# Layer 1's first norm, keys and values of image 0 placed inside layer 0's last image

## The chip, the cores and the metric

The kernel runs as one program on one core of a Trainium2 chip. The metric is the device time of one execution in microseconds (us); less is better. The core's engines each work through their own instructions in program order: TensorE (PE in the profile, with PEld for its weight loads), VectorE (DVE), ScalarE (ACT), GpSimd (POOL) and SyncE (SP, which issues most of the transfers here). They wait for each other by semaphores. Matrix products are written to PSUM, in eight banks; everything else lies in SBUF.

## The reference

Eight images of 256 channels by 32 by 32 pixels go through two layers, all in float32. Layer 0 is a convolutional block, layer 1 a causal attention and a mixture of eight experts over the 1,024 pixels of an image as tokens.

```
# layer 0, per image x [256, 1024]
a = rmsnorm(x) -> 1x1 conv to q, k (4 heads x 32) and v (4 heads x 64), batch norms folded
o = softmax(q.T k) v  +  depthwise 3x3 conv of v
x = x + gamma1 * proj(o)
h = 1x1 conv of rmsnorm(x) to 1024 channels ; depthwise 3x3 conv       # 8 groups of 128 channels
h = gelu(h[:512]) * h[512:]                                              # 4 products of two groups
x = x + gamma2 * irfft2(rfft2(1x1 conv of h to 256) * filter)           # on 8x8 blocks

# layer 1, per image t [1024, 256]
z = layernorm(t)
W = (z WQ.T)(z WK.T).T / 16 ;  A = causal softmax of W, rows where W == 0 left out
t = t + A (z WV.T)
t = t + sum over 8 experts of gate_e * expert_e(layernorm(t))            # two hidden layers, relu
```

## The kernel before

The program has three parts, one after the other: layer 0 for the images 0 to 7, layer 1's attention for the images 0 to 7 (the function `tokens`, its block `l1`), and the experts (its block `l2`). Between layers an image lies in DRAM: `t_d[b]` after layer 0, `u_d[b]` after layer 1's attention.

**How the order is made.** Nearly all instructions go through a small recorder, `InOrder`, with one object for each engine (`pe`, `dve`, `act`, `pool`). It keeps an engine's instructions in the order in which the Python code issues them, so that order is written out by hand: stages are generators that issue a few instructions and yield an estimate in us, and `weave`, `together`, `level`, `some` and `silent` interleave them. All recorded instructions carry the recorder's line, L73; groups in the profile are told apart by the names of their tiles. A stage that is issued earlier stands ahead in every engine's queue.

**Layer 0's opening.** SP issues the loads of the weights and of images 0 and 1. `queries_keys(0)`, `stack(0)` and `values(0)` make image 0's attention inputs, and `queries_keys(1)` those of image 1: TensorE products `pq`, evicted by ScalarE to `hi` and by VectorE to `lo`, both stored to DRAM as `part`. `stack(b)` loads them back into `qst` and `kst`. `hi` and `lo` have one buffer each, so the second half of `queries_keys(1)` waits for the store of the first.

**Layer 0's loop.** For each image i, `main_of(i)` runs image i's attention (`attend`: scores `s`, ScalarE's exponentials `pT`, the products `po` and `sums`), its end (`finish`, which divides by the sums in three steps called turn, back and spread, and `project`, products `pp`), and the spectrum of image i-2. Beside it runs `hidden(i - 1)`, the depthwise convolution of the image before: seven or eight groups of eight taps on VectorE, each tap a 128x1024 multiply-add on `x` or `conv`, after TensorE's products `ph` and ScalarE's evictions of them into a padded tile `hpad`. One group in some images goes over TensorE instead (`group_on_pe`: diagonal weights `taps`, products `pc`).

**Layer 0's end, around the change.** Image 7 has no following attention to hide its second half. After `attend(7)` come: the gelus of image 6 on ScalarE woven with `finish(7)` and `project(7)`, then `head`, which weaves `norm2(7)` (tiles `sq`, `ms`, `yr`, `tpy`, `rbn`, `xn`) with `spectrum(6)` (tiles `pz`, `zf`, `pf`, `gf`, `py`); then image 7's convolution alone (`hidden(7, alone=True)`, group 2 on TensorE), with `scores_matrix` on TensorE at its beginning; each product of two finished groups (`hid`) goes at once into the `pz` accumulators (`mix`). `spectrum(7)` closes the layer, and `votes` and `bad` decide whether a fallback runs (it does not for these inputs).

`scores_matrix` turns the two weights WQ and WK (`lin`), multiplies them into one matrix `pa` and stores it as `at_d`. In the kernel before, `lin` takes over the buffer of `qst` after the last attention.

**Layer 1's start.** `tokens` opens its own pools, loads `t`, `at` and `wv` on GpSimd's queue, and then makes image 0's inputs with nothing beside them:

```python
            for _ in first_norm(0):
                pass
            for _ in keys_values(0):
                pass
            load_t(2)
            for b in range(B):
                together(last() if b == B - 1 else causal(b), beside(b), 0.85)
```

`first_norm` calls `layer_norm`: TensorE transposes `tpt`, ScalarE copies them into `zt`, VectorE's statistics `st` and `mv`, six small GpSimd instructions for the reciprocal root `r`, VectorE's scaling of `zt`, transposes back `tpz`, and ScalarE's copies into `z`. `keys_values` multiplies `z` by `at` (`pk`, copied to `kk`) and by `wv` (`pv`, copied to `v`). `causal(b)` then issues image b's scores `s<-kk,z`, and `beside(b)` the next image's norm, keys and values and the last image's second norm.

The pools have fixed places in SBUF. A tile in a place that another tile has held waits for the old tile's last users.

Of the kernel before, what the change touches and what calls it, by code (L numbers as in the profile page):

```python
# [105 lines left out]
def conv_attn_hybrid_kernel(  # L106
# [370 lines left out]
    t = [None] * B  # L477
    with ExitStack() as l0:
        wpool = l0.enter_context(tc.tile_pool(name="w0", bufs=1))
        one = l0.enter_context(tc.tile_pool(name="one0", bufs=1))  # L480
        two = l0.enter_context(tc.tile_pool(name="two0", bufs=2))
        ps_s = l0.enter_context(tc.tile_pool(name="ps_s0", bufs=2, space=PSUM))
# [41 lines left out]
        sel = two.tile([nf, P], F32, tag="pT", name="sel", bufs=4)  # L524
        nc.sync.dma_start(sel, c_sel)
        fp = two.tile([nf, C], F32, tag="pT", name="fp", bufs=4)
# [6 lines left out]
        nc.sync.dma_start(idft, c_idft)  # L533

# [12 lines left out]
        def spread_columns(w, factors, n):  # L547

            diag = two.tile([P, n, P], F32, tag="pT", name="diag", bufs=4)
            sps = ps_m.tile([P, n, P], F32, tag="mm", name="sps")  # L550
            for g in range(n):
                dve.tensor_scalar_mul(diag[:, g, :], ident, factors[:, g : g + 1])
                pe.matmul(sps[:, g, :], ones, diag[:, g, :], start=True, stop=True)
            for k in range(KC):
                dve.tensor_mul(w[:, k, :], w[:, k, :], sps.rearrange("p a b -> p (a b)"))
# [42 lines left out]
        OTHERS = (0, 1, 2, 3, 5, 6, 7, 8)  # L598

# [125 lines left out]
        def stack(b):  # L725
            for g in range(2):
                hi, lo = att[b][g]
                name = ("qst", "kst")[g]
                att[b][name] = st = one.tile([P, NH, N], F32R, tag=name, name=name)
# [6 lines left out]
        def values(b):  # L736


            vT = att[b]["vT"] = one.tile([P, NT, C], F32, tag="vT", name="vT")
# [36 lines left out]
        def attend(b):  # L776
# [76 lines left out]
            for c in range(N // QC):  # L853
                qs = slice(c * QC, (c + 1) * QC)
                po = ps_o.tile([P, NH // 2, QC], F32, tag="po", name="po")
                sm = ps_o.tile([P, QC], F32, tag="sm", name="sums")
                for j0 in range(0, nj, 2):
                    new = []
                    for j in (j0, j0 + 1):
# [4 lines left out]
                        pT = two.tile([P, NH, QC], F32, tag="pT", name="pT", bufs=4)  # L864
# [13 lines left out]
        def finish(b):  # L878
            for step in att[b]["rest"]:
                step()  # L880
                yield 0.4
# [246 lines left out]
        def main_of(i):  # L1128
# [35 lines left out]
            else:  # L1164
                yield from weave(project(i, (0,)), weave(finish(i), gelus, 1), 1)
                yield from project(i, (1,))
# [19 lines left out]
        for _ in queries_keys(1):  # L1186
            pass
        for i in range(B):


            if i == 0:
                level(main_of(i), v_conv(i), SHARE[0])
            else:
                level(main_of(i), hidden(i - 1, v_conv(i)), SHARE[i])

        lin = one.tile([P, 4, KC, C], F32, tag="qst", name="lin")
        for i, src in enumerate((wqT, wkT)):
            nc.sync.dma_start(lin[:, i], src.rearrange("(k p) o -> p k o", p=P))

        def scores_matrix():  # L1200
            for i in range(2):
                tp = ps_m.tile([P, KC, KC, P], F32, tag="mm", name="tpw")
                for g in range(KC):
                    for k in range(KC):
                        pe.transpose(tp[:, g, k, :], lin[:, i, k, g * P : (g + 1) * P], ident)
                act.copy(lin[:, 2 + i], tp.rearrange("p g k d -> p g (k d)"))
                yield 0.5
            pa = ps_m.tile([P, KC, C], F32, tag="mm", name="pa")
            for g in range(KC):
                for k in range(KC):  # L1210
                    pe.matmul(
                        pa[:, g, :], lin[:, 3, k, g * P : (g + 1) * P], lin[:, 2, k, :], start=(k == 0), stop=(k == KC - 1)
                    )
            act.activation(lin[:, 0], pa, AF.Copy, scale=1.0 / math.sqrt(C))
            nc.sync.dma_start(at_d, lin[:, 0])
            yield 1.7

        head = weave(norm2(B - 1), spectrum(B - 2), 1)
# [3 lines left out]
        def rest():  # L1222
            yield from head
            yield from scores_matrix()
# [20 lines left out]
    def tokens(stack):  # L1245
# [11 lines left out]
        mhalf1 = wm.tile([P, NT], F32, name="mhalf1")  # L1257
        nc.gpsimd.memset(mhalf1, -0.5)
# [44 lines left out]
        def layer_norm(src, dst, zt, room, bank):  # L1303

            n = src.shape[2] // P
            mv = room([P, NT, 2], "mv", 2)
            for i0 in range(0, n, 2):
                tp = bank([P, 2, C], "tpt")
                for i in range(2):
                    for k in range(KC):  # L1310
                        c0 = (i0 + i) * P
                        pe.transpose(tp[:, i, k * P : (k + 1) * P], src[:, k, c0 : c0 + P], ident)
                act.copy(zt[:, i0 : i0 + 2, :], tp)
                yield 0.6
                for i in range(i0, i0 + 2):
                    st = room([P, 6], "st", 4)
                    dve.bn_stats(st, zt[:, i, :])
                    dve.bn_aggr(mv[:, i, :], st)
                yield 0.6

            y = room([P, NT], "y1", 2)[:, :n]
            r = room([P, NT], "r1", 2)[:, :n]
            pool.tensor_scalar(y, mv[:, :n, 1], LN_EPS, None, ALU.add)
            pool.tensor_tensor(r, y, mhalf1[:, :n], ALU.pow)
            pool.tensor_mul(y, y, r)
            pool.tensor_mul(y, y, r)
            pool.tensor_scalar(y, y, -0.5, 1.5, ALU.mult, ALU.add)
            pool.tensor_mul(r, r, y)

            for _ in range(4):  # L1330
                yield 1.0

            def scaled(i0):
                for i in range(i0, i0 + 2):
                    dve.tensor_scalar(zt[:, i, :], zt[:, i, :], mv[:, i, 0:1], r[:, i : i + 1], ALU.subtract, ALU.mult)

            scaled(0)
            yield 1.0
            scaled(2)
            yield 1.0  # L1340
            for i0 in range(0, n, 2):
                if i0 + 4 < n:
                    scaled(i0 + 4)
                tp = bank([P, KC, 2, P], "tpz")
                for i in range(2):
                    for k in range(KC):
                        pe.transpose(tp[:, k, i, :], zt[:, i0 + i, k * P : (k + 1) * P], ident)
                act.copy(dst[:, :, i0 * P : (i0 + 2) * P], tp.rearrange("p k i c -> p k (i c)"))
                yield 0.9

# [30 lines left out]
        with ExitStack() as l1:  # L1381
# [8 lines left out]
            def load_t(b, queue=nc.sync):  # L1390
                t[b] = two.tile([P, KC, N], F32, tag="t", name="t1", bufs=3)
                queue.dma_start(t[b], t_d[b])

            load_t(0, pool)
            at = wpool.tile([P, KC, C], F32, name="at")
            pool.dma_start(at, at_d)
            wv_s = wpool.tile([P, KC, C], F32, name="wv")
            pool.dma_start(wv_s, wvT.rearrange("(k p) o -> p k o", p=P))
            feats[1] = wpool.tile([P, KC, HALF], F32, name="feat1")
            load_t(1)  # L1400


            lower = wpool.tile([P, P], F32, name="lower")
            nc.gpsimd.memset(lower, 1.0)
            nc.gpsimd.affine_select(
                out=lower, in_=lower, compare_op=ALU.is_ge, fill=0.0, base=0, pattern=[[-1, P]], channel_multiplier=1,
            )
# [68 lines left out]
            def rows_of_zt():  # L1476
                return two.tile([P, NT, C], F32, tag="zt", name="zt", bufs=1)

            def first_norm(b):
                z[b] = two.tile([P, KC, N], F32, tag="z", name="z1")  # L1480
                yield from layer_norm(t[b], z[b], rows_of_zt(), room, bank)

            def keys_values(b):
                kk = kk_of[b] = two.tile([P, KC, N], F32, tag="kk", name="kk")
                for h in range(2):
                    hs = slice(h * HALF, (h + 1) * HALF)
                    for g in range(KC):
                        pk = ps_m.tile([P, HALF], F32, tag="mm", name="pk")
                        for k in range(KC):
                            pe.matmul(pk, at[:, k, g * P : (g + 1) * P], z[b][:, k, hs], start=(k == 0), stop=(k == KC - 1))  # L1490
                        act.copy(kk[:, g, hs], pk)
                        yield 1.7
                v = v_of[b] = two.tile([P, NT, C], F32, tag="v", name="v")
                for j in range(0, NT, 2):
                    pv = ps_m.tile([P, 2, C], F32, tag="mm", name="pv")
                    for i in range(2):
                        js = slice((j + i) * P, (j + i + 1) * P)
                        for k in range(KC):
                            pe.matmul(pv[:, i, :], z[b][:, k, js], wv_s[:, k, :], start=(k == 0), stop=(k == KC - 1))
                    act.copy(v[:, j : j + 2, :], pv)  # L1500
                    yield 1.7
# [492 lines left out]
```

## Time and profile before

| | us |
|---|---|
| median of 3 runs | 3138.48 (3132.07 to 3140.57) |
| the profiled execution, its own time | 3137.65 |
| its span, first to last instruction | 3135.9 |
| mean granted TensorE clock | 0.966 |
| TensorE busy | 2944.8 (94%) |
| VectorE busy | 2394.8 (76%) |
| ScalarE busy | 1562.0 (50%) |
| GpSimd busy | 314.2 (10%) |
| last `sums` product of image 7's attention ends | 1241.14 |
| first `ph` product of image 7's convolution starts | 1283.70 |
| last product of two groups (`hid`) of image 7 has its first half done | 1375.26 |
| first score product of layer 1 starts | 1417.46 |

The profile comes from one execution. Times inside it count from its first instruction. A row of the timeline gives start, length, engine, source line, operation, output tile and input tiles, shapes, count, and in square brackets the idle time before the row with what ended it. One float32 matrix product appears as two records, one float32 transpose as one. A row of the table by stages gives, for a stretch of time, the busy us of each engine with the number of its instructions in brackets, the granted TensorE clock as a share of full speed, the busy share of the transfer engines, and GB/s.

### The profile page before, as it was taken

How to read it: one execution, taken by the hardware profiler on the slowest of the kernel's cores; microseconds unless marked ns; L12 is line 12 of the kernel's file. 1: busy time of each engine (PE TensorE's matmuls, PEld its weight loads, DVE VectorE, ACT ScalarE, POOL GpSimd, SP SyncE). 2: the span in 40 equal slices, each digit the busy share in tenths (PEclk: the TensorE clock that was granted, in tenths of full speed). 3: DMA queues.
4: the chain of work that ended last, by engine and by line, in shares of the span. 5: the costliest groups of instructions: out<-in, count | busy, mean ns of one | idle time of the engine just before them, and what ended most of it. 6: DMA issues, size and time to landing. Idle time of an engine off the chain costs nothing.

```text
span 3135.9 us, 41559 instructions
## 1 busy us (share of the span) xinstructions
PE 2944.8 (94%) x16802; PEld 1951.5 (62%) x16802; DVE 2394.8 (76%) x3014; ACT 1562.0 (50%) x2312; POOL 314.2 (10%) x422
## 2 busy tenths in 40 slices
PE   7988999999999988869999999899999999999998
PEld 4554555555555555446666666677777777777776
DVE  2387787878787869576776765688888988888887
ACT  3554454545464545323333333465666666666664
POOL 1012111111111110011122222100000000000000
PEclk8999999999999989989999999999999999999999
DMA  5203030303021210012333311411222142112210
GB/s 181 55 1 81 28 82 28 82 28 79 30 74 36 68 28 8 18 67 71 146 120 131 121 78 54 188 68 68 71 91 74 67 167 107 69 68 77 91 68 28
DMA packets 63600, 234.86 MB, mean 75 GB/s; under 512 B 5591, under 2 KB 13607, under 8 KB 54567
## 3 DMA queue, kind: packets, MB, share of 16 engines
q1 hardware_dynamic: 63094, 230.54, 22.1%
q8 instruction: 134, 2.20, 0.3%
q0 software_dynamic: 304, 1.57, 0.1%
q14 instruction: 68, 0.55, 0.1%
HBM read 140.61 MB, written 91.49 MB: 74 GB/s over the span
## 4 chain that ended last, share of the span: by engine, by line
PE 81%; DVE 13%; ACT 3%; issue 1%; DMA 1%; POOL 1%; SPq 0%; ACTq 0%; DVEq 0%; POOLq 0%
PE pm L73 12%; PE pa L73 11%; PE q L73 11%; PE po L73 11%; PE s L73 8%; PE ph L73 6%; DVE o L73 4%; PE sums L73 3%; PE pq L73 3%; PE pz L73 2%; PE pv L73 2%; PE pk L73 2%; DVE conv L73 2%; PE pp L73 2%; DVE x L73 1%
## 5 line engine op out<-in xcount | busy, mean ns | idle before, releaser
L73 PE MATMUL pa<-ze,w 128*128 128x512 f32 x1488 | 423.1, 393 | 0.0
L73 DVE SCALAR_TENSOR_TENSOR x<-hpad,vec,x 128x1024 f32<-128x1024 f32 x248 | 316.7, 1283 | 76.2 <-ACT x L73 68.7
L73 DVE SCALAR_TENSOR_TENSOR conv<-hpad,vec,conv 128x1024 f32<-128x1024 f32 x256 | 328.5, 1287 | 18.3 <-ACT conv L73 12.3
L73 PEld LDWEIGHTS pa<-ze,w 128*128 128x128 f32 x1488 | 278.2, 188 | 63.2 <-issue 3.0
L73 ACT ACTIVATE h<-pa,bn_o,s1a 128x512 f32<-128x512 f32 x256 | 198.6, 776 | 203.2 <-PE pa L73 203.2
L73 ACT ACTIVATE pT<-s 128x1024 f32<-128x1024 f32 x256 | 247.8, 1024 | 98.5 <-PE s L73 98.5
L73 PE MATMUL po<-pT,vT 128*32 128x256 f32 x4096 | 273.5, 385 | 0.0
L73 PE MATMUL q<-h2p,w 128*128 128x512 f32 x768 | 269.0, 459 | 0.0
L73 DVE SCALAR_TENSOR_TENSOR h<-pa,s1b,h 128x512 f32<-128x512 f32 x256 | 191.5, 748 | 93.9 <-PE pa L73 86.8
L73 PE MATMUL ph<-xn,piw 128*128 128x512 f32 x512 | 240.9, 613 | 7.6 <-ACT x L73 4.0
L73 PE MATMUL pm<-h,w 128*128 128x512 f32 x512 | 240.9, 593 | 0.0
L73 PE MATMUL s<-kk,z 128*128 128x512 f32 x512 | 236.8, 594 | 4.1 <-DVE pr L73 4.1
L73 PE MATMUL q<-z_first,w 128*128 128x512 f32 x768 | 217.2, 391 | 2.8 <-DVE z_first L73 1.7
L73 PE MATMUL pm<-h1p,w 128*128 128x512 f32 x768 | 216.7, 390 | 0.5 <-DVE h1p L73 0.5
L73 PEld LDWEIGHTS q<-h2p,w 128*128 128x128 f32 x768 | 144.6, 188 | 83.2 <-issue 59.6
L73 DVE SCALAR_TENSOR_TENSOR o<-vpad,pe_w,o 128x1024 f32<-128x1024 f32 x128 | 163.7, 1283 | 32.0 <-ACT o L73 28.8
L73 PE MATMUL s<-qst,kst 128*128 128x256 f32 x1024 | 179.0, 320 | 7.0 <-ACT pT L73 4.9
L73 PEld LDWEIGHTS po<-pT,vT 128*32 128x32 f32 x4096 | 120.8, 110 | 85.9 <-issue 5.8
L73 PEld LDWEIGHTS s<-qst,kst 128*128 128x128 f32 x1024 | 142.5, 201 | 44.7 <-issue 30.3
L73 PEld LDWEIGHTS ph<-xn,piw 128*128 128x128 f32 x512 | 93.4, 194 | 121.7 <-issue 99.4
L73 PEld LDWEIGHTS q<-z_first,w 128*128 128x128 f32 x768 | 144.4, 188 | 34.5 <-DVE z_first L73 2.9
L73 PEld LDWEIGHTS pm<-h1p,w 128*128 128x128 f32 x768 | 144.7, 188 | 31.7 <-DVE h1p L73 0.9
(269 smaller groups left out, 5050.6 us busy)
## 6 DMA issues: line engine op xcount, KB each, us to landing
ze<-zd SPq DMA_DIRECT2D x29, 1536.0 KB, 6.5
qst<-part SPq DMA_DIRECT2D x32, 512.0 KB, 9.7
kst<-part SPq DMA_DIRECT2D x32, 512.0 KB, 15.8
te<-ud SPq DMA_DIRECT2D x32, 512.0 KB, 4.1
wd<-parts_w SPq DMA_DIRECT2D x20, 768.0 KB, 3.7
w<-wd SPq DMA_DIRECT2D x20, 768.0 KB, 4.6
zd<-parts SPq DMA_DIRECT2D x14, 1024.0 KB, 3.9
t<-in_x_dram SPq DMA_DIRECT2D x8, 1024.0 KB, 5.1
```

What stands on the lines that cost most here:

```text
L73: return self._tc.keep_in_program_order(method(*args, **kwargs))
```

## The change

1. `scores_matrix` moves from the beginning of image 7's convolution to the opening, directly behind `queries_keys(1)` and ahead of image 0's attention. `lin` is loaded with the first weights and lies in the buffer of `o`.
2. The attention's own tiles (`qst`, `kst`, `vT`, `pT`) get a pool of their own, `own`, which is closed after image 7's attention. In its place a pool `early` is opened with image 0's `z`, `kk`, `v`, a `zt`, two `t` buffers, `at`, `wv` and `lower`. The loads of `t[0]`, `at`, `wv` and `t[1]` are issued there, on SP.
3. The end of image 7's attention takes the order of the other images: all gelus first, then `turn`, `project` half 0, and the rest of `finish` and half 1 of `project` between the first steps of `spectrum(6)`.
4. Image 0's `layer_norm` is woven step by step into `norm2(7)` and `spectrum(6)`; its `keys_values` follow, after a wait of LEAD = 38 in the planner's own us, inside image 7's convolution. Both use the two PSUM banks of the attention's `po` and `sums` in turn.
5. `tokens` begins with image 0's scores. Layer 1's even images use the `early` tiles, the odd ones tiles of its own.

The core of the diff (`layer_norm` and `keys_values` are moved out of `tokens` unchanged, but for the names of the tiles that they are given):

```diff
+        lin = one.tile([P, 4, KC, C], F32, tag="o", name="lin")
+        for i, src in enumerate((wqT, wkT)):
+            nc.sync.dma_start(lin[:, i], src.rearrange("(k p) o -> p k o", p=P))
...
-                att[b][name] = st = one.tile([P, NH, N], F32R, tag=name, name=name)
+                att[b][name] = st = own.tile([P, NH, N], F32R, tag=name, name=name)
...
             else:
-                yield from weave(project(i, (0,)), weave(finish(i), gelus, 1), 1)
-                yield from project(i, (1,))
+                yield from gelus
+                yield from some(finish(i), 1)
+                yield from project(i, (0,))
...
         for _ in queries_keys(1):
             pass
+        for _ in scores_matrix():
+            pass
         for i in range(B):
...
-        lin = one.tile([P, 4, KC, C], F32, tag="qst", name="lin")
...
-        head = weave(norm2(B - 1), spectrum(B - 2), 1)
+        attention.close()
+        early_stack = ExitStack()
+        early = open_early(early_stack)
+        for b in range(2):
+            t[b] = early["t"][b]
+            nc.sync.dma_start(t[b], t_d[b])
+            if b == 0:
+                load_weights(early)
+        turns_of = [0]
+
+        def bank0(shape, name):
+            turns_of[0] += 1
+            return ps_o.tile(shape, F32, tag=("po", "sm")[turns_of[0] % 2], name=name)
+
+        norm0, keys0 = first_tokens(early, bank0, bank0)
+        mixing, second, ends = spectrum(B - 2), norm2(B - 1), finish(B - 1)
+        silent(second, 1)
+        silent(mixing, 1)
+        silent(ends, 1)
+        silent(mixing, 1)
+        silent(ends)
+        silent(mixing, 2)
+        silent(project(B - 1, (1,)))
+        head = weave(weave(second, mixing, 1), norm0, 1)
         while not ready2.get(B - 1):
             next(head)
 
         def rest():
             yield from head
-            yield from scores_matrix()
+            yield from itertools.repeat(1.0, LEAD)
+            yield from keys0
 
         together(rest(), hidden(B - 1, (), (2,), alone=True), 1.0)
...
-            for _ in first_norm(0):
-                pass
-            for _ in keys_values(0):
-                pass
-            load_t(2)
+            z[0], kk_of[0], v_of[0] = (early[name] for name in ("z", "kk", "v"))
+            if not ready_made:
+                for steps in first_tokens(early, bank, bank_kv):
+                    for _ in steps:
+                        pass
```

## The prediction

> **What bounds the kernel now.** The page's first part comes first: TensorE is busy 94% of the span, and the chain that ended last lies on PE for 81% and on DVE for 13%. The change, however, touches three short stretches, and each has a limit of its own. The table by stages shows where that differs:
>
> ```profile
> core 0: us, PE busy (x) PEld busy (x) DVE busy (x) ACT busy (x) POOL busy (x), PEclk, DMA share, GB/s
> 1325.00:1370.00 45.00, 27.27 (x74) 16.38 (x72) 42.05 (x35) 10.36 (x16) 6.05 (x7) 0.81 0.10 35
> 1390.00:1404.00 14.00, 5.58 (x33) 5.28 (x34) 8.77 (x45) 3.93 (x8) 2.75 (x6) 0.76 0.72 262
> 1404.00:1417.00 13.00, 13.00 (x46) 8.55 (x45) 0.00 (x0) 4.57 (x8) 0.00 (x0) 1.00 0.01 1
> ```
>
> Image 7's convolution (1325 to 1370) is VectorE's: 42 of 45 us, with TensorE idle 18. Layer 1's start is a serial chain: 1390 to 1404 belongs to statistics and turns, and in 1404 to 1417 VectorE does nothing while TensorE makes keys and values. The timeline names that chain:
>
> ```profile
> 1390.25 1.94 PE L73 MATMUL tpt<-ident,t 128*128 128x128 f32 x16 [0.66 <-PE votes L1235]
> 1400.36 3.49 PE L73 MATMUL tpz<-ident,zt 128*128 128x128 f32 x16 [8.17 <-DVE zt L73]
> 1403.68 7.03 PE L73 MATMUL pk<-z,at 128*128 128x512 f32 x16
> 1410.55 7.07 PE L73 MATMUL pv<-wv,z 128*128 128x256 f32 x32
> 1417.46 1.88 PE L73 MATMUL s<-kk,z 128*128 128x512 f32 x4
> ```
>
> The votes stand at 1389.40, the first scores at 1417.46. Between them TensorE waits 8.17 us for the norm and then works 17.6 us with nobody beside it. The other two places, the end of image 7's attention with its convolution, and the opening:
>
> ```profile
> 1251.60 6.24 PE L73 MATMUL pp<-o,projw 128*128 128x512 f32 x8 [4.51 <-DVE o L73]
> 1290.15 3.08 PE L73 MATMUL pa<-lin 128*128 128x256 f32 x8 [0.68 <-ACT lin L73]
> 1306.29 15.73 PE L73 MATMUL pc<-vpad,taps 128*128 128x512 f32 x36 [2.15 <-ACT x L73]
> 1326.88 10.53 DVE L73 SCALAR_TENSOR_TENSOR conv<-hpad,vec,conv 128x1024 f32<-128x1024 f32 x8 [6.67 <-ACT conv L73]
> 1338.19 5.64 PE L73 MATMUL pz<-pow__147,hid 128*128 128x256 f32 x16 [9.30 <-DVE hid L73]
> ```
>
> ```profile
> 66.93 1.51 PE L73 MATMUL s<-qst,kst 128*128 128x256 f32 x8
> 69.99 1.94 ACT L73 ACTIVATE pT<-s 128x1024 f32<-128x1024 f32 x2
> 70.72 1.41 DVE L73 SCALAR_TENSOR_TENSOR lo<-pq,qkv_o,hi 128x512 f32<-128x512 f32 x2 [5.27 <-DMA part<-lo]
> ```
>
> I write E for the end of the last sums (1241.14) and F for the first product of image 7's convolution (1283.70).
>
> **Part 1, the opening: +8.5 us (7.1 to 9.5).** In the changed order TensorE has, behind the last pq, the eight turns tpw, the four products pa (eight records), and only then image 0's scores. Each tpw takes a bank in which a pq of queries_keys(1) stood, and that bank is free when VectorE has made lo from it: at 71.45 (70.72 + 1.41/2) and 72.13. Both wait for the store of the earlier lo, which the scores of before did not care about. From there: the second four turns 0.72 (72.85), ScalarE's copy 0.6 (73.45), pa 3.08 by its row, which also followed small gaps (76.5), ScalarE's copy of pa into lin 0.6 (77.1; it stands ahead of the exponentials), the table load 1.28, and the first pT at 78.5 in place of 69.99. The lower end takes pa at 1.72 (four products at 0.43 a record), the upper lets the scores run slowly once after 4.5 us of idle. Behind it TensorE is dense to 130.5, so nothing gives this back. at_d's store (2 us) is done before ScalarE's o, which reuses lin's place, has its turn. The loads of lin (0.5 MB) fall where 0.16 of the transfer engines' time was used (20 to 30 us).
>
> **Part 2, E to F: +2.5 (-0.3 to +5.3).** Now 42.56 us: TensorE idles 1.38 and 4.51, then pp takes 6.24 where eight records take 3.45. The new order puts the first pz behind the last hid (E + 8) and trs, rb, pp half 1 and pf between the pz groups, so the idle time is filled; to be filled in are 16 turns tpt (1.94) and 16 tpz (1.75 at full rate, half the 3.49 shown). Without further waits that is 42.3, a draw. What speaks for more: the scaling zt of the new norm stands ahead of xn on VectorE and waits for six GpSimd instructions (1396.60 to 1399.76, 3.2 us); mv is done at E + 33, zt can start at E + 36.3, the last xn of norm2 is done at E + 43.4, and ph's second half at E + 45.7 instead of some E + 43.5. So +2.2, and 0.3 for the order. The lower end is the walk without that wait; the upper adds one slow spell of 2.8 (6.24 - 3.45) where TensorE had been idle. [...] The trace: after 8.17 us of idle, 3.49 us of nothing but tpz turns at a granted 0.56, and the pk behind them ran at 1.00. [...]
>
> The loads of t[0], at, wv and t[1] move from GpSimd's queue to SP, to E. SP has nothing queued behind them that is due, t lands in about 5 us, and the share of the transfer engines is near 0 from 1250 to 1283: nothing. If that cover were gone, tpt would wait for them, at 5 us per MB. lower's two POOL instructions (0.5 us) now stand ahead of rs, which is due only at E + 3: nothing.
>
> **Part 3, F to the last hid: -2.4 (-4.6 to +1).** Now 91.6 us. Two things change. tpw and pa (5.8 us with their gaps) leave the stretch between the first and second ph; pc can start at F + 18.0 (held then by ScalarE's gelu behind VectorE's first group) instead of F + 22.6, and the two later ph groups come 4.6 earlier. VectorE's 6.67 us wait for conv shrinks to some 2.05: -4.6. Against that, keys0 brings pk and pv, 14.1 us of TensorE, between ph, pc and pz. Most falls in the 18 us of idle that the table shows. But the order is fixed: between group 5's and group 6's ph stand pk, pz, pk and pv, then pv between the halves of group 6; by 1.75 a tile and 3.9 a pz group, group 6's last half is evicted at F + 64.9, where VectorE is free at F + 62.1. A new wait of 1.4 to 2.9; I take 2.2. After that DVE paces again. The upper end (+1) has keys0 meet a granted 0.81, the mean of the stretch, instead of 1.00: 14.1/0.81 is 3.4 more. GpSimd's two sel instructions, which stretch VectorE's hid and conv by 1.7 (2.19 against 1.29, 11.35 against 10.52), stay.
>
> **Part 4, layer 1's start: -27.6 (-28 to -26).** What vanishes is the chain shown above, from the votes' end (1389.6) to 1417.46: 27.9 us. The scores follow the votes at once. In that shadow lay VectorE's small folding instructions (2 us at 1390), two table loads, and the store of image 7's t (issued 1390.17, 3.9 us). The scores take 1.88 + 1.72 themselves, and the exponential comes 5.5 us behind the first score (1423.01 against 1417.46), so the folding fits; I leave 0.3 for it. The store is a new neighbour: the first pr is due 1.1 us after it lands. After that, the order on TensorE (5,664 instructions to the end), SP and the others is the old one, and the added waits name instructions long past.
>
> **Sum** against the profiled execution: 8.5 + 2.5 - 2.4 - 27.6 = -19.0, so 3137.65 - 19.0 = 3118.65. The median is 0.83 above that execution: 3119.5.
>
> **Rivals.**
> - *The opening is hidden* (0.12): the scores matrix costs almost nothing because something late in image 0's attention waited anyway. For it: a 17 us transfer of kst starts at 133.5, behind the attention. Against: that load follows the attention's end. Then -27.5: 3111.
> - *TensorE becomes the bound of image 7's convolution* (0.10): TensorE is busy 64.7 of the 91.6 us now, at a granted 0.87; less tpw and pa (4.3) and with keys0 (14.1) it is 74.5 of 89, which is room, but at 0.75 it would be 74.5 x 0.87/0.75 = 86, and with the waits for VectorE between the pieces more than the stage. Price up to +10: 3129 to 3130.
> - *A wait in layer 1's loop; slower* (0.04). Even images now use the early tiles, odd ones others, and t alternates between two places. If an image's norm waits for the tile's last reader, the price is per image: seven images, and from 19/7 = 2.7 us each it turns the sign. 3.5 us gives 3144. Against it: the order is unchanged, and t is loaded three images ahead (issued some 65 us before use, landing in about 5).
> - *The store of image 7's t is late* (0.04): the transfer engines are full (1.02) at 1396 to 1400, in before for other loads. 5 us: 3124.5.
>
> That the norm, keys and values do not move at all is excluded by the order: they stand ahead of the votes.
>
> **How the numbers follow.** My forecast has 0.70. The sums of the ends are, in parts 1 to 4, -25.8 to -10.2; not all fall together. For 8 in 10 the range runs from 3109 (the hidden opening, with a little more) to 3131 (the TensorE-bound convolution). About 0.3%, 9.4 us, is what a measurement of this kernel can tell from no change: below 3129.1 is faster. Of the forecast and the two milder rivals that leaves 0.87 faster, of the TensorE-bound case and large misses together 0.09 within, and 0.04 slower.
>
> **What would show it.** Opening: first pT at 78.5, tpw waiting for DVE lo. Head: F - E near 45, xn behind zt, zt waiting for POOL r. Convolution: the wait before group 3's conv near 2, one before group 6's conv of 1.4 to 2.9. Start: scores within 0.5 us of the votes, exponential 5.5 behind. Layer 1 and the experts of the same length to 1 us. The prediction is wrong if F to the last hid is over 95 us, if the first pT comes before 73, or if a norm in layer 1 waits for a tile.

## The result and the profile after

The changed kernel takes 3117.55 us (median of 5, 3111.69 to 3121.19), the one before 3137.97 (median of 5). The ratio is 0.9938, with a 95% interval of 0.9921 to 0.9955: 20.4 us faster, where 19.0 were forecast and the range ended at 3109 and 3131. A second set of runs gave 3113.69 (median of 4) and the same ratio, 0.9938 (0.9918 to 0.9957). The profiled execution has a span of 3113.2 us and a time of 3114.98.

The rows that answer to those shown of before, from the same views. First the table by stages (busy us of each engine, granted TensorE clock, transfers):

```profile
core 0: us, PE busy (x) PEld busy (x) DVE busy (x) ACT busy (x) POOL busy (x), PEclk, DMA share, GB/s
1325.00:1370.00 45.00, 36.91 (x112) 23.22 (x112) 38.53 (x32) 14.92 (x23) 3.92 (x3) 0.89 0.00 1
1390.00:1404.00 14.00, 13.64 (x57) 7.69 (x57) 11.06 (x49) 4.03 (x8) 1.41 (x2) 1.00 0.53 189
1404.00:1417.00 13.00, 11.64 (x40) 5.41 (x39) 10.68 (x28) 3.72 (x8) 4.57 (x9) 1.00 0.00 1
```

In 1325 to 1370 TensorE is now busy 36.9 of 45 us instead of 27.3, at a granted 0.89 instead of 0.81, and VectorE only 38.5 instead of 42.1: the keys and values fill TensorE's idle time, but VectorE has got idle time of its own. The other two stretches hold layer 1's work with several engines side by side, where there was one chain before. The timeline, from the votes to the load of the exponential's table, shows the chain gone:

```profile
1393.23 0.19 PE L1363 MATMUL votes<-ones,good 128*1 128x1 f32 x2 [0.17 <-DVE t L73]
1393.35 1.98 PE L73 MATMUL s<-kk_e,z_e 128*128 128x512 f32 x4
1399.30 1.28 ACT L73 ACT_TABLE_LOAD   x1 [0.32 <-DMA td<-t]
```

The scores start 0.12 us behind the votes. The table load is released by the store of image 7's t, the new neighbour that the prediction named. At the end of layer 0's last image, VectorE's rows around the first scalings of the new norm are:

```profile
1280.45 0.73 DVE L73 TENSOR_SCALAR zt_e<-zt_e,mv,r 128x256 f32<-128x256 f32 x2 [1.93 <-POOL r L73]
1282.53 1.40 DVE L73 SCALAR_TENSOR_TENSOR xn<-t,vec,rbn 128x512 f32<-128x512 f32 x2
```

The scaling zt waits for GpSimd's root r, with xn behind it, as forecast. Now image 7's convolution:

```profile
1304.34 17.43 PE L73 MATMUL pc<-vpad,taps 128*128 128x512 f32 x36 [4.11 <-ACT x L73]
1326.62 10.53 DVE L73 SCALAR_TENSOR_TENSOR conv<-hpad,vec,conv 128x1024 f32<-128x1024 f32 x8 [3.85 <-ACT conv L73]
1337.94 6.11 PE L73 MATMUL pz<-pow__152,hid 128*128 128x256 f32 x16 [4.16 <-DVE hid L73]
1354.13 10.53 DVE L73 SCALAR_TENSOR_TENSOR conv<-hpad,vec,conv 128x1024 f32<-128x1024 f32 x8 [3.88 <-ACT conv L73]
```

VectorE's wait before its first conv group (group 4) has shrunk from 6.67 to 3.85, and a new one of 3.88 stands before group 6. Both pc and the first pz follow an idle time of TensorE, of 4.11 and 4.16 us, and are slow: pc takes 17.43 at a granted clock of 0.90, against 15.73 at 1.00 in before, and pz takes 6.11 at 0.60, where a later pz row of this trace (16 records at 1.00) takes 3.62. Rows that take longer than the same row does at a granted clock of 1.00 are called cold from here on, the others warm. And the opening:

```profile
69.22 1.41 DVE L73 SCALAR_TENSOR_TENSOR lo<-pq,qkv_o,hi 128x512 f32<-128x512 f32 x2 [3.31 <-ACT hi L73]
70.03 1.31 PE L73 MATMUL tpw<-ident,lin 128*128 128x128 f32 x8 [2.08 <-DVE lo L73]
72.02 1.99 PE L73 MATMUL pa<-lin 128*128 128x256 f32 x8 [0.68 <-ACT lin L73]
75.96 1.94 ACT L73 ACTIVATE pT<-s 128x1024 f32<-128x1024 f32 x2
```

The turns tpw wait for VectorE's lo, as forecast, but lo itself is released by ScalarE's hi and not by a transfer, and pa takes 1.99.

Where the time went is read from the stretches between landmarks, each in two executions of both kernels (the second ones are the runs e0 and e7 below). E and F are as in the prediction; H is the middle of the last hid row, V the start of the votes, S the first score of layer 1, X its first exponential pr.

| stretch | before | changed | forecast | measured |
|---|---|---|---|---|
| turn tpy of queries_keys(1) to first pT | 19.63, 19.75 | 25.37, 25.54 | +8.5 | +5.8 |
| first pT to image 1's first qst load (end of attention 0) | 60.49, 60.50 | 59.07, 59.05 | 0 | -1.4 |
| to E | 1110.65, 1107.35 | 1107.92, 1106.01 | 0 | none that shows |
| E to F | 42.57, 42.57 | 43.38, 43.49 | +2.5 | +0.9 |
| F to H | 91.50, 91.50 | 92.45, 91.49 | -2.4 | +0.5 |
| H to V | 14.20, 14.19 | 14.45, 14.23 | 0 | +0.1 |
| V to S | 28.06, 28.06 | 0.12, 0.12 | -27.9 | -27.9 |
| S to X | 6.84, 6.84 | 7.25, 7.45 | +0.3 | +0.5 |
| X to the end | 1711.6, 1711.6 | 1712.6, 1711.9 | 0 | +0.6 |

Without the third row, whose means differ by 2.0 us where two executions of before alone differ by 3.3 (e0), the measured column sums to -20.9, close to the medians' -20.4.

### The profile page after: what moved, and what is told of

It is laid out like the page before. It is cut to its first block, busy times and chain, and to the rows that moved or that the text cites. A ratio compares the mean times of both kernels' runs of the same rounds, so it can differ in the third digit from the quotient of the medians.

```text
span 3113.2 us, 41565 instructions
## 1 busy us (share of the span) xinstructions
PE 2935.5 (94%) x16802; PEld 1944.3 (62%) x16802; DVE 2394.0 (77%) x3014; ACT 1562.5 (50%) x2312; POOL 311.1 (10%) x419
## 3 DMA queue, kind: packets, MB, share of 16 engines
HBM read 140.61 MB, written 91.49 MB: 75 GB/s over the span
## 4 chain that ended last, share of the span: by engine, by line
PE 81%; DVE 13%; ACT 3%; DMA 1%; issue 1%; POOL 1%; SPq 0%; ACTq 0%; DVEq 0%
PE pm L73 12%; PE pa L73 11%; PE q L73 11%; PE po L73 11%; PE s L73 8%; PE ph L73 6%; DVE o L73 4%; PE pq L73 3%; PE sums L73 3%; PE pz L73 2%; DVE x L73 2%; PE pv L73 2%; PE pk L73 2%; PE pp L73 2%; DVE conv L73 1%; DVE zt_e L73 1%
## 5 line engine op out<-in xcount | busy, mean ns | idle before, releaser
L73 PE MATMUL sums<-pT,ones 128*32 128x256 f32 x2048 | 157.4, 379 | 0.0
```

The lines of the kernel that those rows point to most:

```text
L73: return self._tc.keep_in_program_order(method(*args, **kwargs))
```

## The experiments

**e0: what two executions differ by.** The kernel before, once more.

> The kernel before, a second execution, to see what two executions of one kernel differ by. In the first one the last sums ended at 1241.14, and in the changed kernel at 1242.95, although its first exponential came 5.97 later: 4.2 us were lost on the way, 1.4 of them by the end of image 0's attention (130 us). Theory A: those 2.7 us between 130 and 1241 are what executions differ by. Then this one ends its last sums up to some 3 us from 1241.14 as well, and drifts against the first one between images. Theory B: the loop gives the delay back. Then this one stays within 0.5 us of the first one at 1241.

It took 3134.74 us, and its last sums ended at 1238.22. The opening, and all that follows E, agree with the first execution to 0.4 us; the difference, 3.3 us, arises between 130 and 1241. Over all eleven traces of this study this stretch, with nearly the same instructions, takes 1102.6 to 1110.7 us, and it goes with TensorE's clock: the shortest have a mean granted clock of 0.97 and 1018 us of busy PE, the longest 0.95 and 1034. Theory A stands: the 4.2 us that the changed kernel seemed to win back on its way to E are 1.4 in image 0's attention (there before was granted 0.73 in 70 to 75, the changed kernel 1.00 in 76 to 81) and otherwise what executions differ by. So single times are not compared here for differences of a few us; the stretches are.

**e1: the scores matrix alone in the opening.** The kernel before, with

```diff
+        lin = one.tile([P, 4, KC, C], F32, tag="o", name="lin")   # loaded with the first weights
...
         for _ in queries_keys(1):
             pass
+        for _ in scores_matrix():
+            pass
...
-            yield from scores_matrix()                             # in rest()
```

> The kernel before with the first part of the change alone: the scores matrix is made in the opening, the rest is as before. Theory: the first exponential comes at 76 to 78.5 instead of 69.99 (by how long the store of the earlier lo takes), image 0's attention ends 4.5 to 6 later, and that stays. F to the last hid (first half) 88.7 instead of 91.6: the diagonal group starts 4.6 us earlier but, behind an idle time of 4.1, runs cold and takes 17.4 instead of 15.7, so that VectorE's wait before group 4 is 3.8. Rival, the prediction's term: that wait is 2.05 and the stretch takes 87.0. Time 3137.65 + 4.5 - 2.9, about 3139.5.

The time was 3146.29 us, 6.8 more than expected. The first pT came at 78.77, 28.21 behind tpy and 8.5 later than in before, which is more than the 76 to 78.5 expected and most of the miss: here the matrix ran cold (tpw 1.80, pa 3.78 and the first scores 1.92, where the changed kernel shows 1.31, 1.99 and 1.30 at a granted 1.00):

```profile
73.04 3.78 PE L73 MATMUL pa<-lin 128*128 128x256 f32 x8 [0.68 <-ACT lin L73]
78.77 1.94 ACT L73 ACTIVATE pT<-s 128x1024 f32<-128x1024 f32 x2
```

So the opening's price was 5.4 to 5.9 us in five traces and 8.5 in this one, in which the matrix ran cold. F to H took 89.74: the wait before group 4 was 5.22, because pc, starting at F + 18.07 as forecast, took 18.80. My 88.7 was 1 us too low, the prediction's own 87.0 2.7 too low; the direction (pc runs cold) holds. E to F was 42.60, as in before.

**e2: the order without the norm.** The changed kernel, with

```diff
-        head = weave(weave(second, mixing, 1), norm0, 1)
+        head = weave(second, mixing, 1)
...
-            yield from itertools.repeat(1.0, LEAD)
-            yield from keys0
...
+        silent(norm0)              # behind the votes
+        silent(keys0)
```

> The changed kernel, but with image 0's norm, keys and values issued behind the votes instead of inside image 7's convolution (the matrix in the opening and the new order of image 7's end stay). Theory: the turns and scalings of the norm cost E to F about 2 us, so F - E is 40.5 to 41.5 (43.4 with them, 42.6 before). Rival: the new order itself gains nothing and F - E stays at 43. F to the last hid 88.7, without the wait before group 6 (3.88 with the keys and values; theory: keys and values cause all of it); rival: the wait stays near 3.9 and the stretch takes 92. First scores 27.5 to 28.5 behind the votes. Time 3114.98 + 27.9 - 2 - 3.7, about 3137.

It took 3128.57 us. E to F is 38.71: the new order of image 7's end is worth 3.9 us by itself, and the norm puts 4.7 to 4.8 back. Both were more than expected. F to H is 86.95, with 3.85 before group 4 (as in the changed kernel) and no wait before group 6: keys and values make that one. Of the 4.55 us against before, 2.82 are the shorter wait, and 1.7 come from something that I had not foreseen: GpSimd's sel instructions, beside which VectorE's hid or conv are longer in the other kernels (a hid of 2.89 us instead of 1.29 in the changed kernel), stand behind the norm's GpSimd part here and fall behind the votes. There they met the scalings zt instead:

```profile
1386.16 0.94 POOL L1489 MEMSET sel<- 32x1024 f32 x1
1386.26 5.69 DVE L73 TENSOR_SCALAR zt_e<-zt_e,mv,r 128x256 f32<-128x256 f32 x8 [2.37 <-POOL r L73]
1387.18 2.24 POOL L1491 TENSOR_SCALAR_AFFINE_SELECT sel<-sel 32x1024 f32<-32x1024 f32 x2
```

The eight scalings took 5.69 us, where before has 2.67 for them, and V to S was 30.32, 2.3 longer than in before and longer than expected. With the short stretch to E (1102.59) and the two gains ahead of H the time is less than the 3137 expected.

**e3: the matrix where TensorE waits anyway.** The changed kernel, with

```diff
-        for _ in queries_keys(1):
-            pass
-        for _ in scores_matrix():
-            pass
+        steps = queries_keys(1)
+        silent(steps, 4)
+        silent(scores_matrix())
+        silent(steps)
```

> The changed kernel, but with the scores matrix issued inside the norm of queries_keys(1), between the turns tpy and tr, where TensorE waits 3.67 us for GpSimd's root, instead of behind the last pq. Theory: the matrix costs the opening its whole 5.97 because it stands between pq and the first scores and waits for lo; in the gap it is free, and pq, which runs cold there (9.26 for 16 records, 7 at full rate), gains up to 2. First exponential at 68 to 70.5 instead of 75.96. Rival: the tr turns get later by as much as the matrix takes (banks, ScalarE's copies), so the exponential comes at 73 or later. Time by the theory 6 us less than the changed kernel: 3109 beside 3115, 3111.5 for the median.

Median 3113.49 us of 4 (ratio to before 0.9925, 0.9908 to 0.9941), where 3111.5 was expected. The first pT came 21.13 behind tpy: 4.3 of the 5.8 us are gone. Not all, because in the gap the matrix runs cold (tpw 1.91, pa 3.53 against the changed kernel's 1.31 and 1.99), and GpSimd's root no longer decides when the turns tr start (56.98 instead of 54.94 in the changed kernel's):

```profile
51.02 1.91 PE L73 MATMUL tpw<-ident,lin 128*128 128x128 f32 x8
53.61 3.53 PE L73 MATMUL pa<-lin 128*128 128x256 f32 x8 [0.68 <-ACT lin L73]
71.68 1.94 ACT L73 ACTIVATE pT<-s 128x1024 f32<-128x1024 f32 x2
```

The exponential lies between the two expectations, a little nearer to the theory's. The whole time does not show the gain: the interval of the ratio overlaps that of the changed kernel, and two later stretches of this trace were longer. F to H took 94.04, with pc at 18.78, and X to the end 1715.8, 3.2 to 3.9 more than in the changed kernel; there, in layer 1's image 1, 1484.63 to 1494.63 and 1494.63 to 1504.63 were granted 0.79 and 0.87, where before has 1.00 at the same place (1514.30 to 1534.30). In e6 and e8, which make the matrix at the same place, the first pT came 22.76 and 23.02 behind tpy.

**e4: the tiles of keys0 placed by hand.** The changed kernel, with

```diff
-            yield from itertools.repeat(1.0, LEAD)
+            yield from itertools.repeat(1.0, 17)
+            silent(keys0, 2)
+            yield from itertools.repeat(1.0, 22)
+            silent(keys0, 5)
+            yield from itertools.repeat(1.0, 10)
             yield from keys0
```

> The changed kernel, but keys0's eight tiles are placed by hand: two ahead of the diagonal group's pc (where TensorE waits 4.1 us), five ahead of the first pz (where it waits 4.2), one behind group 6's ph; nothing of them is left between the first pz and that ph. Theory: the two cold spells and the tiles between the halves of group 6's ph make the waits of 3.85 and 3.88. So pc takes 15.5 to 16 instead of 17.4, VectorE's wait before group 4 is 2.1 to 2.4, the first pz takes 3.6 instead of 6.1, the wait before group 6 is gone, and F to the last hid is 86.5 to 87.5 instead of 92.45. Rival: the waits are set by ScalarE's queue or by banks, not by TensorE's order: the stretch stays at 90 or more.

It took 3115.07 us, with a stretch to E of 1109.88, a slow stretch in the opening (32 products thr in 5.87 us, 3.93 in the changed kernel) and another behind E (E to F 45.19, with the changed kernel's instructions; 1258 to 1268 was granted 0.85 and 1286 to 1293.96 0.79, where the changed kernel has 1.00 throughout). The convolution did what the theory said, F to H in 86.77:

```profile
1311.97 15.73 PE L73 MATMUL pc<-vpad,taps 128*128 128x512 f32 x36 [0.68 <-ACT x L73]
1332.56 10.53 DVE L73 SCALAR_TENSOR_TENSOR conv<-hpad,vec,conv 128x1024 f32<-128x1024 f32 x8 [2.16 <-ACT conv L73]
1343.87 3.89 PE L73 MATMUL pz<-pow__152,hid 128*128 128x256 f32 x16 [0.69 <-DVE hid L73]
1356.10 10.52 DVE L73 SCALAR_TENSOR_TENSOR conv<-hpad,vec,conv 128x1024 f32<-128x1024 f32 x8
```

pc has its 15.73 us again, pz 3.89, the first wait is 2.16, and group 6 (at 1356.10) has none. The same work in another order takes 4.7 to 5.7 us less: TensorE's order and the two idle times ahead of pc and pz made those waits. The changed kernel's own trace speaks against ScalarE's queue as well: ScalarE waits there 1.19 us for TensorE's ph just ahead of group 6. Banks were not varied by themselves.

**e5: the scalings behind xn.** The changed kernel, with layer_norm issuing all eight scalings zt in one go, LEAD 34, and

```diff
-        head = weave(weave(second, mixing, 1), norm0, 1)
+        head = weave(weave(second, mixing, 1), some(norm0, 12), 1)
...
             yield from head
+            silent(norm0, 2)
+            yield 0.1
+            yield from norm0
```

> The changed kernel, but VectorE's eight scalings zt of image 0's norm stand behind the last xn of norm2, and the turns tpz behind the first ph products. Theory: the norm costs E to F what it does (43.38 against 38.71 without it) because the scalings wait for GpSimd's root ahead of xn: F - E is then 40 to 41. Rival: TensorE's turns tpt and the statistics cost it: F - E stays at 42.5 or more. F to the last hid within 1 us of 92.45, since VectorE waits 4 us there for the first taps and the scalings take 2.9.

It took 3114.18 us, and E to F 40.02: the scalings ahead of xn, with the turns tpz behind them, were 3.4 of the norm's 4.7 us. VectorE's rows at that place:

```profile
1285.53 1.40 DVE L73 SCALAR_TENSOR_TENSOR xn<-t,vec,rbn 128x512 f32<-128x512 f32 x2
1286.86 2.67 DVE L73 TENSOR_SCALAR zt_e<-zt_e,mv,r 128x256 f32<-128x256 f32 x8
1290.84 9.21 DVE L73 SCALAR_TENSOR_TENSOR x<-hpad,vec,x 128x1024 f32<-128x1024 f32 x7 [1.31 <-ACT x L73]
```

The scalings fill the idle time ahead of the first taps. F to H became 93.69, a little past the 1 us that I allowed: with the keys shifted, the wait before group 6 was 5.83. Together, E to H is 1.3 to 2.1 us shorter than in the two traces of the changed kernel.

**e6 and e8: all three together.** e6 joins e3, e5 and a placing like e4's (two tiles ahead of pc); e8 leaves the room ahead of pc empty:

```diff
+            yield from itertools.repeat(1.0, 35)
+            silent(keys0, 5)
+            yield from itertools.repeat(1.0, 10)
             yield from keys0
```

> The changed kernel with all three: the scores matrix in the gap of the norm, the scalings behind xn, the tiles of keys0 placed by hand. Theory, by the segments of the traces: the first exponential at 71.7 (75.96 in the changed kernel), F - E 40.5 (43.4), F to the last hid 87 (92.45), the rest as before: some 13 us less than the changed kernel, 3104 for the median where executions of the changed one have 3117.5. Rival: the savings don't add, because the norm's tail collides with the first keys, F to the last hid 90 or more; then 3108.

> As the run with all three, but none of keys0's tiles stands ahead of pc: five stand between group 5's ph and the first pz, where TensorE waited 9.3 us without them, two behind group 6's ph, one behind the second pz. Theory: what went wrong there was pc, which waited until 22.0 behind the first ph for the pk ahead of it (18.0 to 19.2 elsewhere); the wait before group 4 is 3.3 as with the late scaling alone, the one before group 6 is gone, so F to the last hid is 87 to 88 (90.6 with all three, 93.7 with the late scaling alone), F - E 40.1. Rival: the late turns of the norm cost the convolution as much as they save before it: 89.5 or more. By the theory the median is 3108 to 3111, some 6 less than the changed kernel.

e6: median 3113.17 us of 4 (ratio 0.9925, 0.9908 to 0.9942), E to F 40.15, F to H 90.63: the savings did not add up, as the rival said, though its 3108 was missed too. The first pT was 22.76 behind tpy, and X to the end 1715.7, next to e3's 1715.8. e8: median 3108.90 of 5 (3104.00 to 3112.24), ratio 0.9912 (0.9898 to 0.9925), the lowest median here and 4.8 to 8.7 us below the two medians of the changed kernel, whose ratio of 0.9938 has intervals that just overlap with this one. E to F was 40.86 and F to H 91.67. The median is where the theory had it, but that is in part luck, since F to H, the stretch that it was about, missed: my 87 to 88 was wrong and the rival's 89.5 or more held. The tiles ahead of pc were not the whole reason: in both, the first ph ran cold, 5.37 us at a granted 0.57 to 0.58 in e6 and 5.72 at 0.50 for its first 4 us in e8, where e5, with the same instructions in the same order between E and there, has 3.67 at 1.00:

```profile
1281.55 5.72 PE L73 MATMUL ph<-xn,piw 128*128 128x512 f32 x8
1302.80 17.38 PE L73 MATMUL pc<-vpad,taps 128*128 128x512 f32 x36 [2.15 <-ACT x L73]
1348.58 10.53 DVE L73 SCALAR_TENSOR_TENSOR conv<-hpad,vec,conv 128x1024 f32<-128x1024 f32 x8
```

The wait before group 6 is gone (1348.58). The slow ph makes everything up to pc 2 us later than in e5, and pc at 17.38 instead of 15.73 makes the wait before group 4 4.93 instead of 3.28; these 3.7 us are most of what was missing. Why these two rows were granted less than e5's is open.

**e7: the changed kernel again**, for a second trace and a second median.

> The changed kernel again, on the chip and with the runs of before that the others of this call have. Theory: the first exponential at 76 to 79, F - E 43.4, F to the last hid 92 to 94 and the first score 0.12 behind the votes, as in its first execution, while the stretch between the end of image 0's attention and E differs by several us (1102.6 to 1110.7 in six traces so far). Median 3115 to 3119.

Median 3113.69 us of 4 (3111.60 to 3123.96); its stretches stand in the table. F to H is half a us below what was expected and the median 1.3; the rest held.

## Why the prediction was right, step by step

The forecast of -19.0 became -20.4 (medians) and -20.9 (stretches). Direction, place of the gain and total were right; that the total came so near is in part luck, since the terms missed by up to 3 us, with both signs.

- **Layer 1's start, -27.6.** Right: V to S -27.94 in both traces of the changed kernel. The prediction misread one row: its 1423.01, "5.5 us behind the first score", is the start of the table load, and the first pr of before comes 6.84 behind the score. The 0.3 us were set aside for VectorE's folding, and the store of image 7's t was to land 1.1 us before it is needed; instead the store decides when the table is loaded (the load waits 0.32 and 0.52 us for it), and S to X is 0.4 to 0.6 longer. X to the end is 0.3 to 1.0 longer: in the changed kernel's first trace 1490.6 to 1500.6, in image 1 of layer 1, was granted 0.83, where before has 1.00 at the same place (1514.3 to 1524.3). In e1 the stretch is 0.5 longer too, though it has none of the early tiles.
- **The opening, +8.5.** The mechanism (the scores matrix ahead of the scores, waiting for lo) is what the rows show, but the term was mis-sized: +5.8 in the table, below the stated 7.1, and 5.4 to 5.9 in five of the six traces with the matrix there, 8.5 in e1. Two entries of the sum were off: lo stood at 71.45 because in before it waited for a store, and it came at 69.9; and pa was taken at its slow 3.08 (granted 0.62) where it took 1.99 (at 1.00). The lower end of 7.1 should have dropped the store too. The rival that the opening is hidden falls: no later stretch can be seen to give it back, apart from the 1.4 us in image 0's attention, and e1 has its whole 8.5 us still at E (1249.78 against 1241.13, with 1110.53 to E against 1110.65).
- **E to F, +2.5.** Measured +0.9. I wrote "a draw" for the new order with its turns and +2.2 for the scalings ahead of xn. e2 and e5 give -3.9 for the order, +1.3 for the turns tpt and the statistics, and +3.4 for the scalings with the turns tpz. The wait was named rightly and was dearer; the idle time that the new order fills was undervalued. The first ph, behind the turns tpz, ran at a granted 1.00 in both executions of the changed kernel (32 records in 13.90): no slow spell came there. (Over the tpz row of before, 1400.36 to 1403.85, the granted clock is 0.54, not 0.56.)
- **F to H, -2.4.** This is the step that failed in sign: +0.5. The wait before group 4 ("group 3's conv" in the prediction's signs) was to become 2.05 and became 3.85 and 3.58; the one before group 6 was to be 2.2 and was 3.88 and 3.19. The failed entries are durations: pc was taken at 15.73 and the first pz at 3.9, from rows behind other idle times (the first pz of before, behind 9.30 us, had already taken 5.64, at a granted 0.65). In both traces of the changed kernel pc now follows an idle time of 4.1 us and the first pz one of 4.2, and both are cold (17.43 and 17.16, 6.11 and 5.42). With that idle time filled (e4) the first wait is 2.16, next to the 2.05 of the sum. The part's range of -4.6 to +1 held.
- **The rivals.** No wait in layer 1's loop: X to the end differs from before by 1 us at most in both traces of the changed kernel, and the 4 us more in e3 go with a lower granted clock (0.79 and 0.87 in image 1, 1.00 in before); where e6's 4 us lie is not shown. Behind the same waits for zt (1.67 and 0.48 us), po takes 3.20 for 16 records in before and 3.79 for 15 in the changed kernel's first trace, where 1496 to 1500 was granted 0.57: the difference is in po, not in a wait for a tile. TensorE did not become the bound of the convolution either, although its share rose (27.3 to 36.9 of the 45 us from 1325).

What followed TensorE's idle times in the convolution: pc behind 4.10 to 4.11 us took 17.16 (e7), 17.43 (the changed kernel) and 18.78 (e3), 1.43 to 3.05 more than its warm 15.73, and 16 records of pz behind 4.15 to 4.16 us took 5.42 (e7), 6.11 (the changed kernel), 6.32 (e5) and 6.35 (e3), where warm rows take 3.62 to 3.89. Shorter idle times had a cold row behind them too in some executions: pc behind 2.15 to 2.16 us took 17.38 in e8 and 15.73 in e5 and before, and 16 records of pz behind 2.70 to 2.72 us took 3.89 in before, 5.58 in e4 and 5.17 in e6. So no run here shows a least idle time, and why one row behind the same idle time differs between executions is open.

## What to carry to other kernels

A chain with nothing beside it is worth its full length when its inputs are ready early: that stretch came out within 0.1 us of its 27.9. The price lies where the moved work lands: look there for instructions that have to wait (the scalings for GpSimd) and now stand ahead of others that need not, and for idle times on TensorE, since durations from warm rows did not hold behind them here: behind 4.1 to 4.2 us pc took 17.16 to 18.78 instead of 15.73 and pz 5.42 to 6.35 instead of 3.62 to 3.89, and behind 2 to 3 us they were cold in some executions (e8, e4, e6). With moved work placed inside those idle times pc took 15.73 and pz 3.89 (e4: 4.7 to 5.7 us less in the convolution), but in e6 and e8, where the stretch ahead of it was changed as well, the first ph ran cold (5.37 and 5.72 instead of 3.67) and most of that gain was lost.

## What the runs showed of the hardware that was not expected

- One program's stretch of 1,100 us varied by 8 us from execution to execution with the granted clock (0.95 to 0.97), while VectorE's busy time in it varied by 0.6 us. In the opening, 32 products thr took 3.73 us in e3, 3.93 in the changed kernel (granted 0.93), 4.15 in before (0.88) and 5.87 in e4.
- The store of the first lo was waited for until 4.8 to 5.3 us after its issue in both traces of before and in e3, e6 and e8, where ScalarE's table load follows directly on hi; in the changed kernel, where the table load comes 5 us later, it had landed by 3.3 us. Why is open; it wasn't tried.
- VectorE's instructions beside GpSimd's memset and two selections on a 32x1024 tile were longer: hid and conv by 1.7 us in before (2.19 instead of 1.29, 11.35 instead of 10.52) and hid by 1.6 in the changed kernel (2.89 instead of 1.29). In e2, where they fell beside the scalings zt, hid and conv have 1.29 and 10.53, and the scalings took 5.69 instead of 2.67.
